# Gathered graph convolution: lists in pieces of 64 places for any set of 32-column groups, and half tiles on alternating pairs of banks

## The chip, the cores and the metric

The kernel runs on one core of a Trainium2 chip. The metric is the device time of one execution in microseconds; the time before is the median of three runs, 1504.62 us (1504.0 to 1505.56).

## The reference

`x` is [8, 4096, 256], `adj` [4096, 4096], `W` [256, 256], all float32.

```python
HW = jnp.einsum('bnf,fo->bno', H, W)
A_norm = jax.nn.relu((A + A.T) * 0.5)
D = jnp.sum(A_norm, axis=1)
D_safe = jnp.where(D > 0, D, 1.0)
d_inv_sqrt = jnp.where(D > 0, D_safe ** (-0.5), 0.0)
DAD = d_inv_sqrt[:, None] * A_norm * d_inv_sqrt[None, :]
L_norm = jnp.eye(N, dtype=H.dtype) - DAD
out = jnp.einsum('nm,bmo->bno', L_norm, HW)
return jax.nn.relu(out)
...
x = _layernorm(x + _L0_gnn_ref(x, L0_gnn_W, adj), axis=-1)
```

`adj` is sparse, with a density that falls with the row number: the first rows and columns hold most of the entries. Of the product with the Laplacian, only those rows matter that have an entry in the output block's columns.

## The kernel before, in words

**First stage (to about 582 us).** `adj` is read in blocks of 512 x 512, each is transposed (L515), added to its mirror (L519), put through a relu (L523) and stored in `a_dram`. For each row and each group of 32 columns a flag is kept (`uses`, L527) that says whether there is an entry. Beside that the product of x and W is formed (L615, L626) and stored in `g_dram`, one row of 2048 floats (8 batches x 256), 8 KB, for each node. Output block 0 is accumulated along the way (`lead`, L584). Lists for the first units are made here too.

**Second stage (from 582 us).** The remaining 31 blocks of 128 output columns are taken in 16 units of two blocks (b = 0 and 1; the last unit has one), in the order SEQ. A unit has eight groups of 32 columns, and the set of groups that a row has entries in is its mask, a number from 0 to 255. A unit needs the rows whose mask is not 0. They are placed in list tiles of 128 places, made of two halves of 64; KINDS gives fifteen masks that a half can stand for (single groups, pairs of groups, a whole block, and 0 for everything, "the rest"), CAPS how many halves each gets, FIRST where they begin. A row whose own kind is full goes to a wider one (`offer`, L334 on). For each tile POOL issues two indirect DMAs: the rows' piece of `a_dram`, 32, 128 or 256 columns wide (`ga`, L1031), and their rows of `g_dram` (`g`, L1039). Twelve tiles fit into SBUF (the ring); their slots are given back in the order of issue. The rows of the first 256 nodes, in which nearly all groups have entries, are not gathered: tiles 0 and 1 of `g_dram` are kept in SBUF (`g_hub`), and a unit with HUBS = 2 uses both, one with HUBS = 1 the first alone; their piece of `a_dram`, 64 KB, is loaded for each block (`gh`).

**The products (L1254).** A block's output is [128 columns, 2048], four PSUM banks c = 0 to 3 of 512 each, tag b0 or b1. `steps_of` plans a unit as a sequence of steps. A step fills the 128 columns of TensorE's array: one product of 128 x 128, or several narrower ones of different tiles beside each other; SHAPES lists the widths, and with 64 rows instead of 128 two products share the rows of the array, where half i always writes block i. In each step all products of bank 0 are issued, then those of bank 1, and so on. When block 0 of a unit is complete, `finish` evicts it (ACT, L787), adds the residual (DVE, L797), takes the moments (L806, L808), the inverse root and the normalisation (L830), and stores it.

**The lists** of the units to come are made in passing: `patterns` (L255 to L295) makes the masks and the indicator of each kind, 14 kinds x 32 node blocks = 448 columns; `count` (L299, L300) multiplies them on TensorE with a matrix of ones and a triangle, which gives each row's number within its kind; `place` (L302 to L390) turns it to a place; `count_rest` and `place_rest` (L395 to L419) do so for what is left over; `spread` (L428 to L444) and `collect` (32 small matmuls, L449) turn rows with places into places with rows, and `index` makes the addresses. `lists(u, room)` runs at the end of each unit's block 0: it takes three PSUM tiles of tag b0, issues the counts on TensorE for the third and fourth unit ahead, and the collect matmuls of the second ahead a few at a time between the steps (`thread`).

`queue(engine)` puts an instruction behind the last one issued on that engine, so the order of the program is the order on each queue.

## Time and profile before

| what | before |
|---|---|
| median of 3 runs (range) | 1504.62 us (1504.0 to 1505.56) |
| profiled execution (its span) | 1504.0 us |
| first stage / second stage | 582 us / 922 us |
| TensorE busy in the second stage | 867.87 us |
| VectorE busy in the second stage | 626.69 us |
| GpSimd busy in the second stage | 589.24 us |
| DMA share in the second stage | 0.94 |
| gathers (queue 0) | 53552 packets, 287.25 MB |

In the page, a group of instructions is one line of the program on one engine with its operands, count, busy time, mean time of one (ns) and the idle time of the engine just before. "PE" is TensorE, "PEld" its weight loads, "DVE" VectorE, "POOL" GpSimd. The chain is followed back from the last instruction to what released it, step by step, so its shares say what ended last, not what was busy. In the table of windows each engine has its busy time with the number of instructions in brackets, then TensorE's granted clock, the DMA share and the rate.

### The profile page before, as it was taken

How to read it: one execution, taken by the hardware profiler on the slowest of the kernel's cores; microseconds unless marked ns; L12 is line 12 of the kernel's file. 1: busy time of each engine (PE TensorE's matmuls, PEld its weight loads, DVE VectorE, ACT ScalarE, POOL GpSimd, SP SyncE). 2: the span in 40 equal slices, each digit the busy share in tenths (PEclk: the TensorE clock that was granted, in tenths of full speed). 3: DMA queues.
4: the chain of work that ended last, by engine and by line, in shares of the span. 5: the costliest groups of instructions: out<-in, count | busy, mean ns of one | idle time of the engine just before them, and what ended most of it. 6: DMA issues, size and time to landing. Idle time of an engine off the chain costs nothing.

```text
span 1504.0 us, 20175 instructions
## 1 busy us (share of the span) xinstructions
PE 1406.1 (93%) x6584; PEld 746.6 (50%) x6584; DVE 1028.0 (68%) x3020; ACT 369.3 (25%) x462; POOL 741.5 (49%) x1521
## 2 busy tenths in 40 slices
PE   7998998989999999989898989998999998999996
PEld 6777876767777764323333333333333333333342
DVE  4667579789597734147566776787989239999535
ACT  4555554544445440010100001001010010101102
POOL 2434010011223346756556776676666647567652
PEclk9999999989999999999999999999999999999999
DMA  9999999998999999969889999989999979999995
GB/s 359 349 377 380 402 390 358 394 362 319 400 358 332 364 418 367 377 263 362 338 304 358 334 393 349 373 336 396 413 380 357 408 278 395 382 383 404 409 389 207
DMA packets 215008, 545.83 MB, mean 363 GB/s; under 512 B 16983, under 2 KB 106647, under 8 KB 179879
## 3 DMA queue, kind: packets, MB, share of 16 engines
q0 software_dynamic: 53552, 287.25, 49.1%
q1 hardware_dynamic: 93200, 126.62, 24.3%
q10 hardware_dynamic: 68144, 130.58, 22.7%
q8 instruction: 55, 0.90, 0.2%
q14 instruction: 57, 0.47, 0.1%
HBM read 426.33 MB, written 136.34 MB: 374 GB/s over the span
## 4 chain that ended last, share of the span: by engine, by line
PE 60%; DVE 19%; DMA 12%; issue 5%; ACT 3%; POOL 1%; another core or an unknown queue 0%; ACTq 0%; DVEq 0%; POOLq 0%
PE py L1254 40%; PE pg L626 9%; DMA a_dram<-sym 7%; PE lead L584 5%; DVE sym L519 4%; DMA g<-g_dram,gi 3%; PE xtr L615 3%; PE tr L515 3%; ACT sym L523 2%; DVE stats L806 1%; DVE sums L526 1%; DVE hot L428 1%; DVE xr L830 1%; DVE xr L797 1%; DMA xin<-in_x_dram 1%
## 5 line engine op out<-in xcount | busy, mean ns | idle before, releaser
L1254 PE MATMUL py<-g,ga 128*128 128x512 f32 (+4 forms) x2808 | 678.4, 605 | 23.0 <-issue 16.1
L1254 PEld LDWEIGHTS py<-g,ga 128*128 128x128 f32 (+4 forms) x2808 | 236.6, 140 | 427.5 <-issue 401.1
L1039 POOL DMA_INDIRECT g<-g_dram,gi x257 | 297.4, 1157 | 149.4 <-issue 77.3
L1031 POOL DMA_INDIRECT ga<-a_dram,ai x257 | 269.6, 1049 | 159.8 <-issue 61.2
L787 ACT ACTIVATE y<-py,minus_r 128x512 f32<-128x512 f32 x120 | 80.4, 689 | 807.4 <-PE py L1254 644.7
L626 PE MATMUL pg<-w_sb,xt 128*128 128x256 f32 x1024 | 231.0, 384 | 7.1 <-ACT xt L616 7.1
L626 PEld LDWEIGHTS pg<-w_sb,xt 128*128 128x128 f32 x1024 | 195.3, 193 | 34.2 <-ACT xt L616 8.1
L519 DVE TENSOR_TENSOR sym<-tr,adj 128x512 f32<-128x512 f32 x256 | 162.4, 685 | 57.6 <-PE tr L515 51.2
L526 DVE TENSOR_REDUCE sums<-sym 128x64 f32<-128x2048 f32 x64 | 145.7, 2282 | 65.9 <-ACT sym L523 65.9
L1254 PE MATMUL py<-g_hub,gh 128*128 128x512 f32 x384 | 182.5, 616 | 5.5 <-issue 3.4
L527 POOL TENSOR_SCALAR uses<-sums 128x64 uint8<-128x64 f32 x64 | 26.7, 417 | 268.3 <-DVE sums L526 238.6
L515 PE MATMUL tr<-ident,adj 128*128 128x128 f32 x1024 | 136.9, 281 | 20.7 <-DVE sym L519 14.8
L523 ACT ACTIVATE sym<-sym 128x2048 f32<-128x2048 f32 x64 | 122.8, 1919 | 122.9 <-DVE sym L519 114.2
L515 PEld LDWEIGHTS tr<-ident,adj 128*128 128x128 f32 x1024 | 115.5, 143 | 51.1 <-DVE sym L519 32.1
L1254 PEld LDWEIGHTS py<-g_hub,gh 128*128 128x128 f32 x384 | 71.6, 194 | 111.7 <-issue 104.4
L241 DVE TENSOR_TENSOR_SCAN incl_r<-carry,lists 128x32 f32<-128x32 bf16 x13 | 2.8, 218 | 150.7 <-PE lists L396 147.1
L428 DVE TENSOR_TENSOR hot<-iota_q,at 128x1024 bf16<-128x1024 f32 x64 | 74.5, 1219 | 34.2 <-ACT y L787 32.1
L797 DVE TENSOR_TENSOR xr<-xr,y 128x2048 f32<-128x2048 f32 x31 | 70.8, 2284 | 39.6 <-ACT y L787 36.1
L615 PE MATMUL xtr<-ident,xin 128*128 128x128 f32 x512 | 74.0, 297 | 16.0 <-DVE sym L519 10.0
L830 DVE TENSOR_SCALAR xr<-xr,mv,root 128x256 f32<-128x256 f32 x248 | 85.5, 417 | 1.1
L806 DVE BATCH_NORM_STATS2 stats<-xr 128x6 f32<-128x256 f32 x248 | 84.0, 412 | 1.1
L584 PE MATMUL lead<-gt,strip 128*128 128x512 f32 x176 | 82.4, 593 | 0.0
(164 smaller groups left out, 1032.1 us busy)
## 6 DMA issues: line engine op xcount, KB each, us to landing
adj<-in_adj_dram SPq DMA_DIRECT2D x64, 1024.0 KB
a_dram<-sym ACTq DMA_DIRECT2D x64, 1024.0 KB
out_dram<-xr SPq DMA_DIRECT2D x31, 1024.0 KB
xr<-in_x_dram ACTq DMA_DIRECT2D x28, 1024.0 KB
xin<-in_x_dram SPq DMA_DIRECT2D x44, 512.0 KB
g_dram<-gt ACTq DMA_DIRECT2D x22, 1024.0 KB
xin<-in_x_dram POOLq DMA_DIRECT2D x20, 512.0 KB
g_dram<-held ACTq DMA_DIRECT2D x10, 1024.0 KB
```

What stands on the lines that cost most here:

```text
L515: ins = nc.tensor.transpose(pt[:, c * P : (c + 1) * P], tji[:, c, a * P : (a + 1) * P], ident)
L519: nc.vector.tensor_add(sym[:, a, :], pt, tij[:, a, :])
L523: nc.scalar.activation(sym, sym, AF.Relu, scale=0.5)
L526: nc.vector.tensor_reduce(sums, sym.rearrange("p a (c q) -> p a c q", q=E), AX.X, ALU.add)
L584: nc.tensor.matmul(lead[c], lhsT=strip, rhs=g[:, c * S : (c + 1) * S], start=not done, stop=len(done) == NB - 1, skip_group_check=True,)
L615: nc.tensor.transpose(pt[:, k, c, :], xin[b // H][:, b % H + k, c * P : (c + 1) * P], ident)
L626: ins = nc.tensor.matmul(pg[:, k * FO : (k + 1) * FO], lhsT=xt[:, b + k, c, :], rhs=w_sb[:, c, :], start=(c == 0), stop=(c == FC - 1),)
L806: nc.vector.bn_stats(stats[:, b, :], z[:, b, :])
L830: nc.vector.tensor_scalar(z[:, b, :], z[:, b, :], mv[:, b, 0:1], rstd[:, b : b + 1], ALU.subtract, ALU.mult,)
L1031: nc.gpsimd.indirect_dma_start(out=at if both else at[:, : E if one else P], out_offset=None, in_=a_pairs if both else a_groups if one els ...
L1039: nc.gpsimd.indirect_dma_start(out=gt, out_offset=None, in_=g_dram, in_offset=bass.IndirectOffsetOnAxis(ap=gi[:, t : t + 1], axis=0), boun ...
L1254: return nc.tensor.matmul(py[2 * u + 1 + b][c][cols, :], lhsT=at[ps, off + cols.start : off + cols.stop], rhs=gt[ps, c * S : (c + 1) * S], ...
```

## The change

The lists get a table of their own for each unit. PIECES names, in the order of the places, masks of any kind and how many halves of 64 each has; ORDER gives the sequence in which a unit's tiles are used. `Table` makes from them the kinds, the rest, and for each tile the width of its piece of `a_dram`. `choose` compares each row's mask with all masks of the table (up to 23) and takes the narrowest that holds it; the cascade of offers and the indicator with 448 columns go, and `count` is one matmul with at most 23 columns instead of two with 448. HUBS is 2 for all units. `spread` and `collect` leave out the hub rows (30 instead of 32 matmuls). `lists` takes one PSUM tile instead of three for the counts and the collected lists. Ring slots are given back in any order.

The planner puts products in full rounds ("F", 128 rows) and half rounds ("H", 64 rows, up to eight products beside each other, of any block). Half rounds are issued in groups of up to two. Each has two phases: in the first, products of one row half write banks 0 and 1 and those of the other write banks 2 and 3; in the second it is the other way round. Ahead of the second phases of a group an instruction on TensorE's queue waits for all half products so far. So two halves may now write the same block.

Counted in the program: list tiles 257 to 272, steps 226 to 211 (a half round of two phases counted as one), products of the second stage 1596 to 3472, half rounds 9 to 64 (52 of them with eight products to a bank), waits between phases 0 to 45.

```diff
-KINDS = [15, 1, 4, 2, 8, 16, 64, 32, 128, 240, 51, 204, 60, 195, 0]
...
-HUBS = [2, 2, 2, 1, 2, 2, 2, 1, 1, 2, 1, 1, 1, 1, 2, 2]
+HUBS = [2, 2, 2, 2, 2, 2, 2, 2, 2, 2, 2, 2, 2, 2, 2, 2]
...
+PIECES = [
+    [
+        (154, 2), (69, 2), (245, 2), (209, 1), (232, 1), (175, 1), (64, 2), (2, 3), (41, 2), (43, 1), (195, 1),
...
+ORDER = [
+    [8, 7, 19, 14, 6, 1, 13, 0, 20, 17, 21, 22, 5, 24, 10, 12, 4, 23, 16, 18, 2, 15, 9, 3, 11],
...
+    class Table:
+
+        def __init__(self, u):
+            full = 255 if blocks(u) == 2 else 15
+            self.pieces, at = [], {}
+            for mask, n in PIECES[u]:
+                if mask:
+                    at[mask] = len(self.pieces), n
+                self.pieces += [mask] * n
+            self.pieces += [0] * (len(self.pieces) % 2)
+            self.tiles = len(self.pieces) // 2
+            self.rest = at.pop(full)
+            self.kinds = [(m, *at[m]) for m in sorted(at, key=lambda m: (bits(m), m))]
+            self.places = [self.place(t, u) for t in range(self.tiles)]
+
...
+        def place(self, t, u):
+
+            a, b = self.halves(t)
+            a, b = a or b, b or a
+            if bits(a) == bits(b) == 1:
+                return E, [QU * (2 * u + 1) + m.bit_length() - 1 for m in (a, b)]
+            if all(not m & 15 or not m >> QU for m in (a, b)):
+                return P, [2 * u + 1 + int(not m & 15) for m in (a, b)]
+            return 2 * P, [u, u]
+
+    tables = [Table(u) for u in range(NU)]
...
+    def choose(u):
+
+        pat = plan[u]
+        n = len(tables[u].kinds)
+        ks = slice(kind_at[u], kind_at[u + 1])
+        all_ = [P, n, NB]
+        beyond = ipool.tile([P, kmax, NB], I16, tag="beyond", name=f"beyond_{u}", bufs=1)[:, :n]
+        nc.vector.tensor_tensor(
+            beyond,
+            pat.unsqueeze(1).to_broadcast(all_),
+            outside[:, ks].unsqueeze(2).to_broadcast(all_),
+            ALU.bitwise_and,
+        )
+        kind = ipool.tile([P, kmax, NB], BF16, tag="kind", name=f"kind_{u}", bufs=1)[:, :n]
+        nc.vector.scalar_tensor_tensor(
+            kind, beyond, 0.0, rank[:, :n].unsqueeze(2).to_broadcast(all_), ALU.is_equal, ALU.mult
+        )
+        best = ipool.tile([P, NB], F32, tag="best", name=f"best_{u}", bufs=1)
+        nc.vector.tensor_reduce(best, kind.rearrange("p k m -> p m k"), AX.X, ALU.max)
+        nc.vector.tensor_scalar(best, best, 1.0, None, ALU.max)
+        nc.vector.tensor_tensor(kind, kind, best.unsqueeze(1).to_broadcast(all_), ALU.is_equal)
...
+        plan[u] = pat, kind, incl, tot
...
+    def rounds_of(tiles, nb):
+
+        pend = [(t, set(cells_of(m0, m1, nb))) for t, m0, m1 in tiles]
+        rounds = []
+        while any(left for _, left in pend):
+            near = [p for p in pend if p[1]][:REACH]
+            wide, half = {}, {}
+            for p in near:
+                for b, e, k in sorted(p[1]):
+                    if k == 2:
+                        wide.setdefault(e, (p, b, e))
+                    else:
+                        half.setdefault((k, e), (p, b, e))
+            split = {e: wide[e] for e in wide if (0, e) not in half and (1, e) not in half}
+
+            def oldest(cells):
+                return 0.13 * any(p is near[0] for p, _, _ in cells)
+
+            score = len(wide) / QU + oldest(wide.values())
+            score_h = (len(half) + 2 * len(split)) / (2 * QU) if half else 0
+            score_h += oldest([*half.values(), *split.values()])
+            score_h -= 0.05 * (not rounds or rounds[-1][0] != "H")
+            if wide and score >= score_h:
+                for p, b, e in wide.values():
+                    p[1].discard((b, e, 2))
+                rounds.append(("F", [(p[0], None, b, e) for p, b, e in wide.values()]))
                 continue
+            cells = []
+            for (k, _), (p, b, e) in half.items():
+                p[1].discard((b, e, k))
+                cells.append((p[0], k, b, e))
+            for p, b, e in split.values():
+                p[1].discard((b, e, 2))
+                cells += [(p[0], k, b, e) for k in range(2)]
+            rounds.append(("H", cells))
+        return rounds
+
...
+    def phases_of(u, turn):
+
+        out = []
+        for kind, run in groupby(sequence(u), lambda r: r[0]):
+            run = list(run)
+            if kind == "F":
+                out += [(2, [(op, (0, 1, 2, 3)) for op in ops_of(cells, True)], False) for _, cells in run]
+                continue
+            for k in range(0, len(run), GROUP):
+                group = [ops_of(cells, False) for _, cells in run[k : k + GROUP]]
+                for back in range(2):
+                    for ops in reversed(group) if back else group:
+                        chunks = [(0, 1) if op[1] == turn[0] else (2, 3) for op in ops]
+                        out.append((1, list(zip(ops, chunks)), back == 1 and ops is group[-1]))
+                    if not back:
+                        turn[0] = 1 - turn[0]
+        return out
...
         def gather_ahead():
-            nonlocal asked, eaten
-            while eaten < asked and not uses_left[order[eaten]]:
-                eaten += 1
-            while asked < len(order) and asked - eaten < RING:
+            nonlocal asked
+            while asked < len(order) and free:
                 gather(asked)
                 asked += 1
...
         def lists(u, room):
 
-            tot, low, pr = (psum.tile([P, S], F32, tag="b0", name=f"lists{k}_{u}") for k in range(3))
-            tot, low = tot[:, : NL * NB], low[:, : NL * NB]
-            pl = pr[:, 2 * NB :]
-            pr = pr[:, : 2 * NB].rearrange("p (k m) -> p k m", k=2)
+            pl = psum.tile([P, S], F32, tag="b0", name=f"lists_{u}")
+            low, pr = pl[:, :kmax], pl[:, kmax : kmax + 2]
+            pl = pl[:, P:]
             reads = []
             with queue("pe"):
                 if 3 in ahead[u]:
-                    count_rest(ahead[u][3], pr[:, 0], pr[:, 1])
-                    reads.append(place_rest(ahead[u][3], pr[:, 0], pr[:, 1]))
+                    count_rest(ahead[u][3], pr[:, 0:1], pr[:, 1:2])
                 if 4 in ahead[u]:
-                    count(ahead[u][4], tot, low)
-                    reads.append(place(ahead[u][4], tot, low))
+                    n = len(tables[ahead[u][4]].kinds)
+                    count(ahead[u][4], low[:, :n])
+                    reads.append(place(ahead[u][4], low[:, :n]))
+            if 3 in ahead[u]:
+                in_turn(place_rest, ahead[u][3], pr[:, 0:1], pr[:, 1:2])
             for steps in reads:
                 in_turn(next, steps, None)
             if 2 in ahead[u]:
                 v = ahead[u][2]
-                pl = pl[:, : 2 * tiles[v]].rearrange("p (k t) -> p k t", k=2)
+                t = tables[v].tiles
+                pl = pl[:, : 2 * t].rearrange("p (k t) -> p k t", k=2)
...
+        def wait_for(products):
+
+            with queue("pe"):
+                mark = nc.tensor.nop().ins
+            for ins in products:
+                tc.add_manual_dep(
+                    mark,
+                    ins.name,
+                    mybir.DependencyInfo(mybir.DependencyClass.Sync, mybir.DependencyReason.DATA),
+                    reason="row tiles change banks",
                 )
 
...
+            if fresh:
+                wait_for(halves)
+                halves.clear()
+            first = [op for op, _ in ops if op[2] not in begun]
+            assert not first or [op[1:2] + op[3:] for op, _ in ops] == [(None, 0, QU)]
+            begun.update(touched)
+            for k in range(len(ops[0][1])):
+                for op, cs in ops:
+                    c = cs[k]
+                    for e in range(op[3], op[3] + op[4]):
+                        left[op[2], e, c] -= 1
+                    ends = all(not left[op[2], e, c] for e in range(op[3], op[3] + op[4]))
+                    ins = product(u, op, c, op in first, ends)
+                    if op[1] is not None:
+                        halves.append(ins)
+            for op, _ in ops:
                 t = op[0]
-                uses_left[u, t] -= 1
-                if t < 0:
-                    load_hub_rows(SEQ[SEQ.index(u) + 1 :], -1 - t, op[2])
```

TensorE, in unit 2 of the program (py_2 is that unit's accumulator: unit, block, bank; g and ga are the ring slots). Before, half products of four steps, where the first half writes block 0 and the second block 1:

```order
L1254 MATMUL py_2_0_0_6394<-g9_5749,ga9_5767 32x512 [waits DMASW1_49,DMASW0_49]
L1254 MATMUL py_2_1_0_6531<-g9_5749,ga9_5767 32x512
L1254 MATMUL py_2_0_0_6394<-g10_5753,ga10_5768 32x512 [waits DMASW4_49,DMASW3_49]
L1254 MATMUL py_2_1_0_6531<-g10_5753,ga10_5768 32x512
L1254 MATMUL py_2_0_0_6394<-g11_5757,ga11_5769 32x512 [waits DMASW6_49,DMASW5_49]
L1254 MATMUL py_2_1_0_6531<-g11_5757,ga11_5769 32x512
L1254 MATMUL py_2_0_0_6394<-g0_5713,ga0_5758 32x512 [waits DMASW7_49,DMASW0_49]
L1254 MATMUL py_2_1_0_6531<-g0_5713,ga0_5758 32x512
```

After, the last bank pair of a first phase, then (behind six collect matmuls, cut here) the second phase, whose first product has the wait ahead of it:

```order
L1231 MATMUL py_2_1_1_6639<-g8_5802,ga8_5823 32x512
L1231 MATMUL py_2_1_1_6639<-g5_5790,ga5_5820 32x512
L1231 MATMUL py_2_1_1_6639<-g11_5814,ga11_5826 32x512
L1231 MATMUL py_2_1_1_6639<-g8_5802,ga8_5823 32x512
...
L1231 MATMUL py_2_1_0_6638<-g2_5778,ga2_5817 32x512 [waits PE_49]
L1231 MATMUL py_2_1_0_6638<-g5_5790,ga5_5820 32x512
L1231 MATMUL py_2_1_0_6638<-g11_5814,ga11_5826 32x512 x2
L1231 MATMUL py_2_1_2_6640<-g8_5802,ga8_5823 32x512
L1231 MATMUL py_2_1_2_6640<-g5_5790,ga5_5820 32x512
L1231 MATMUL py_2_1_2_6640<-g11_5814,ga11_5826 32x512
```

Both halves now write block 1, in different banks, and the exchange of banks stands behind a wait on TensorE itself.

TensorE at the end of a unit's block 0, where the lists of later units are counted and collected. Before:

```order
L395 LDWEIGHTS ones
L395 MATMUL lists_2_6659<-rest_6369,ones 128x32 [waits Activation_49]
L396 LDWEIGHTS lower
L396 MATMUL lists_2_6659<-rest_6369,lower 128x32
L299 LDWEIGHTS ones
L299 MATMUL lists_2_6657<-kind_5986,ones 128x448 [waits Activation_49]
L300 LDWEIGHTS lower
L300 MATMUL lists_2_6658<-kind_5986,lower 128x448 [waits Activation_49]
L449 LDWEIGHTS hot_6384 [waits DVE_49]
L449 MATMUL lists_2_6659<-val_6386,hot_6384 128x36 [waits DVE_49]
```

After:

```order
L402 LDWEIGHTS lower_86
L402 MATMUL lists_2_6937<-tot_r_5_6536,lower_86 128x1 [waits Activation_49]
L403 LDWEIGHTS ones_87
L403 MATMUL lists_2_6937<-tot_r_5_6536,ones_87 128x1
L369 LDWEIGHTS lower_86
L369 MATMUL lists_2_6937<-tot_6_6636,lower_86 128x15 [waits DVE_49]
L454 LDWEIGHTS hot_4_6548
L454 MATMUL lists_2_6937<-val_4_6550,hot_4_6548 128x36 [waits DVE_49]
```

The wide counts are gone, and the first collect matmul now writes the tile that VectorE reads the counts from.

VectorE at the same place, ahead of which the collect matmul waits. Before:

```order
L241 SCALAR_TENSOR_TENSOR incl_r6_7120<-carry_96,lists2_3_7115 128x32 [waits PE_49]
L245 TENSOR_TENSOR pos_r6_7122<-incl_r6_7120,lists2_3_7115 128x32 [waits DVE_49]
L246 TENSOR_TENSOR pos_r6_7122<-pos_r6_7122,lists2_3_7115 128x32 [waits DVE_49]
L241 SCALAR_TENSOR_TENSOR incl_k7_7125<-carry_96,lists0_3_7113 128x448 [waits PE_49]
L245 TENSOR_TENSOR pos_k7_7127<-incl_k7_7125,lists0_3_7113 128x448 [waits DVE_49]
L246 TENSOR_TENSOR pos_k7_7127<-pos_k7_7127,lists1_3_7114 128x448 [waits DVE_49,PE_49]
L797 TENSOR_TENSOR xr_7_7006<-xr_7_7006,y_7_7092 128x2048 [waits DMAHW4_49,DMAHW0_49,Activation_49]
```

After:

```order
L409 TENSOR_SCALAR over_125<-lists_2_6937 128x1 [waits PE_49]
L410 TENSOR_SCALAR incl_r_5_6534<-incl_r_5_6534,lists_2_6937 128x32
L412 SCALAR_TENSOR_TENSOR fits1_5_6943<-incl_r_5_6534,rest_5_6532 128x32 [waits DVE_49]
L413 SCALAR_TENSOR_TENSOR incl_r_5_6534<-incl_r_5_6534,fits1_5_6943 128x32 [waits DVE_49]
L414 TENSOR_TENSOR slot_5_6528<-slot_5_6528,incl_r_5_6534 128x32 [waits DVE_49]
L416 TENSOR_SCALAR ip_5_6947<-slot_5_6528 128x32 [waits DVE_49]
L420 TENSOR_SCALAR digit_5_6949<-ip_5_6947 128x32 [waits DVE_49]
L421 CAST at_5_6950<-digit_5_6949 128x32 [waits DVE_49]
L422 TENSOR_SCALAR digit_5_6949<-ip_5_6947 128x32 [waits DVE_49]
L423 CAST at_5_6950<-digit_5_6949 128x32 [waits DVE_49]
L378 TENSOR_TENSOR at_k_6_6955<-lists_2_6937,base_101 128x15
```

Before, the tile of the rest and of the collected lists (lists_2) had its last reader in the third operation; after, the one tile has it in the eleventh.

657 lines of the change are left out of this document (278 added, 379 removed), and 47 rows, old and new, of tables (CAPS, FIRST, ORDER).

## The prediction

> **What bounds the kernel now.** I read the page first, for the span and the busy shares, then the table of windows for the two stages, and then the chain of what ended last in three stretches of the second stage.
>
> ```profile
> span 1504.0 us, 20175 instructions
> PE 1406.1 (93%) x6584; PEld 746.6 (50%) x6584; DVE 1028.0 (68%) x3020; ACT 369.3 (25%) x462; POOL 741.5 (49%) x1521
> q0 software_dynamic: 53552, 287.25, 49.1%
> ```
>
> ```profile
> core 0: us, PE busy (x) PEld busy (x) DVE busy (x) ACT busy (x) POOL busy (x), PEclk, DMA share, GB/s
> 0.00:582.00 582.00, 538.22 (x2893) 420.61 (x2894) 401.36 (x768) 280.55 (x328) 152.22 (x967) 0.97 1.00 371
> 582.00:1504.00 922.00, 867.87 (x3693) 325.99 (x3691) 626.69 (x2252) 88.78 (x134) 589.24 (x555) 0.97 0.94 358
> ```
>
> The span is the profiled execution's whole time; the median of the timed runs, 1504.62 us, lies 0.6 us above it, and I add that at the end. In the first stage (to 582 us) the DMA engines are busy for 1.00 of the time, so what the change does there to TensorE and VectorE is hidden; I take that stage as it is. In the second stage TensorE is busy for 867.87 of 922 us and the DMA share is 0.94: two limits that are only 54 us apart. The chain tells which of them ends last, by stretches (582 to 922, 922 to 1262, 1262 to 1492):
>
> ```profile
> by line: PE py L1254 92.1%; issue 5.4%; PE lists L449 1.3%; PE lead L584 0.4%; DVE incl_r L241 0.3%; DVE pos_r L245 0.3%; DVE pos_r L246 0.3%; PE lists L396 0.1%; PE lists L395 0.1%
> ```
>
> ```profile
> by line: PE py L1254 51.8%; DMA g<-g_dram,gi 6.2%; DVE hot L428 4.0%; DVE stats L806 4.0%; DVE xr L830 4.0%; issue 3.7%; DVE xr L797 3.3%; another core or an unknown queue 1.1%; DVE incl_k L241 0.9%; DVE slot L386 0.8%; DVE mv L808 0.8%; DV
> ```
>
> ```profile
> by line: PE py L1254 47.1%; DMA g<-g_dram,gi 11.4%; issue 10.0%; POOL g L1039 4.8%; POOL ga L1031 3.7%; DMA ga<-a_dram,ai 2.9%; DVE stats L806 2.5%; DVE xr L830 2.4%; DVE hot L428 2.0%; DVE xr L797 1.9%; PE lists L449 0.7%; DVE g L1108 0.5%
> ```
>
> So the units that run up to 922 us are bound by the products of TensorE; behind that, products hold about half of the chain and the rest is split between VectorE and the gathers. A TensorE term counts in full at first and less later.
>
> **Part by part: steps and half tiles.** A step of four full products is eight matmul records in a row; where two of them stand between pieces of other work, each takes 3.52 us, and a step in which each quarter of the columns is another tile's costs the same. The windows hold single steps, in this order: eight half products to a bank (two rows), six to a bank, four quarter products of 128 rows (two rows).
>
> ```profile
> 648.09 3.52 PE py L1254 x8
> 651.62 0.27 PE lists L449 x11
> 651.89 3.52 PE py L1254 x8
> ```
>
> ```profile
> 636.51:643.12 6.61, 6.40 (x65) 1.65 (x64) 0.00 (x0) 1.85 (x3) 1.95 (x2) 1.00 0.77 316
> 713.59:718.53 4.94, 4.82 (x65) 1.62 (x64) 0.00 (x0) 1.85 (x3) 0.94 (x1) 1.00 1.02 428
> 847.17:850.75 3.58, 3.58 (x50) 1.01 (x48) 0.00 (x0) 0.93 (x2) 2.70 (x3) 1.00 0.94 329
> 855.80:859.38 3.58, 3.58 (x34) 1.66 (x29) 3.44 (x4) 0.00 (x0) 2.73 (x3) 1.00 0.88 295
> 643.12:646.69 3.57, 3.57 (x34) 0.94 (x32) 0.00 (x0) 0.69 (x1) 0.00 (x0) 1.00 0.00 0
> ```
>
> From the two planners' tables I count 226 steps before and 211 after (a half round of two phases counted as one step, hub steps included), with 14 more hub steps among the 211: 15 steps fewer at 3.53 us is **-53 us**. In exchange the after kernel has 64 half rounds where the before had nine, and 52 of the 64 have eight half products to a bank. Their price is the open size of this case. The six-op row says 3.58 us, nothing extra; the two eight-op rows say 1.37 and 3.04 us extra. In both of these the first two of the four banks run at full pace, then a few records come about 0.7 us apart, and then the pace is full again. The chain shows the same crawl from 666 us on, in a step of 128-row quarter products and the hub step behind it, so it is not proven to belong to half products:
>
> ```profile
> 638.98 2.06 PE py L1254 x7
> 641.04 0.12 issue
> ...
> 666.17 0.10 issue
> 666.27 0.59 PE py L1254
> 666.86 0.12 issue
> 666.98 0.61 PE py L1254
> 667.59 0.85 issue
> 668.44 0.59 PE py L1254
> ```
>
> I take 0.5 us for each of the 52, a good third of the smaller of the two rows, since the row of six stands at nothing: **+26 us**, with ends 0, +71 (1.37 each) and +158 (3.04 each).
>
> The Trainium skill speaks to this on the page "TensorE: Matmul & The Clock Gate", section "Packing small matmuls — row/col tiling": tiles of the array that don't collide overlap within its 64-deep window, and a pack takes one matmul's time plus about 4 ns for each further tile. By that rule the 26 us would be zero; the six-op row agrees, the two eight-op rows do not.
>
> **The waits between phases.** Each group of half rounds (45 of them, 26 with one round and 19 with two) gets an instruction on TensorE's queue that waits for all half products issued so far, before the row halves swap their pairs of banks. Behind it are queued that group's remaining products, the list matmuls threaded between them, and so the eviction and the release of ring slots. A wait of this kind is not in the trace. From below stand the short "issue" pieces of the chain (0.10 to 0.12 us above), from above one of them plus one matmul that has to run out, 605 ns by the mean of the products' row:
>
> ```profile
> L1254 PE MATMUL py<-g,ga 128*128 128x512 f32 (+4 forms) x2808 | 678.4, 605 | 23.0 <-issue 16.1
> L1254 PE MATMUL py<-g_hub,gh 128*128 128x512 f32 x384 | 182.5, 616 | 5.5 <-issue 3.4
> ```
>
> I take 0.4 us, the middle, 45 times: **+18 us** (5 to 32). Switching between full and half rows is in that figure.
>
> On the page "TensorEngine Tiling (Array Packing)", section "Key Properties", the Trainium skill says that a change of tiling mode, not only of the tile, drains the TensorE. That speaks against a change that switches so often; but the step of 3.57 us in the windows' last row starts where the eight-op step of the first row ends, and it is no longer than the other of its kind, so no such drain shows here.
>
> **The list machinery.** Two 448-column count matmuls per unit go (12 units) for one of at most 23 columns: 24 x 0.35 us = **-8.4 us**. But all parts of a unit's lists now share one PSUM tile, so the first collect matmul waits for VectorE's last reader of that tile, and products queue behind it on TensorE. Before, three short operations stood there:
>
> ```profile
> L300 PE MATMUL lists<-kind,lower 128*128 128x448 bf16 x12 | 4.2, 350 | 0.0
> ...
> L418 DVE TENSOR_SCALAR digit<-ip 128x32 int32<-128x32 int32 x13 | 2.7, 207 | 2.7 <-DVE at L417 2.4
> L410 DVE TENSOR_TENSOR slot<-slot,pos_r 128x32 f32<-128x32 f32 x13 | 2.5, 196 | 3.1 <-DVE pos_r L407 2.8
> ```
>
> ```profile
> 722.32 0.23 DVE incl_r L241
> 722.57 0.20 DVE pos_r L245
> 722.79 0.20 DVE pos_r L246
> 722.99 0.04 issue
> ```
>
> That is 0.63 us. After, ten operations of place_rest and one of place stand there, of the kinds that take 0.16 to 0.21 us: about 2.3 us, 1.7 more, 13 times: **+22 us**. Below it could be 0 where VectorE is done long before TensorE arrives; above it could be 13 x 3.7 = 48, if each grows to the longest wait of this kind that there is now:
>
> ```profile
> PE lists L449 <- DVE pos_r L246: 11.8, 11, 4.3
> ```
>
> The 448-column operations on VectorE are fewer and the cascade of offers goes:
>
> ```profile
> L241 DVE TENSOR_TENSOR_SCAN incl_k<-carry,lists 128x448 f32<-128x448 bf16 x12 | 13.0, 1080 | 0.3 <-PE lists L300 0.3
> L386 DVE TENSOR_REDUCE slot<-pos_k 128x32 f32<-128x448 f32 x12 | 11.1, 928 | 0.4
> L383 DVE TENSOR_TENSOR pos_k<-pos_k,fits 128x448 f32<-128x448 f32 x12 | 7.6, 630 | 0.4
> ```
>
> Before, a unit's lists take a scan, a reduction and six operations of 448 columns by these rows (5.8 us), and the half-width and small ones of the cascade and the patterns, some 17 us as I estimate it; after, about seven operations of up to 22 x 32 elements at 0.6 to 0.7 us, a scan of 1.1, two reductions of 1.0 and the small ones, some 11 us: 12 x 6 = 70 us less busy. VectorE holds about a fifth of the chain in the middle stretch and less than that in the last, so I count a fifth: **-14 us** (0 to -30).
>
> **Transfers.** Fifteen more tiles, but pieces of 64 places let 703 fewer rows be gathered (30,655 to 29,952 counted from the input, 8 KB each, 5.76 MB). Queue 0 spends 49.1% of 1504 us on 287.25 MB, 2.57 us a MB: -14.8 us; 14 hub loads of 64 KB (0.9 MB) give 2.4 back. Of 12.4 us I count half, as the gathers end last only in the later stretches: **-6 us** (0 to -12). Two more POOL issues for each of 15 tiles cost what these rows say:
>
> ```profile
> L1039 POOL DMA_INDIRECT g<-g_dram,gi x257 | 297.4, 1157 | 149.4 <-issue 77.3
> L1031 POOL DMA_INDIRECT ga<-a_dram,ai x257 | 269.6, 1049 | 159.8 <-issue 61.2
> ```
>
> 15 x 2.2 = 33 us beside 589 busy of 922: hidden while ring slots are free; without that cover they cost their 33. Slots now come free in any order, so an early half tile no longer holds back those behind it; what that gains is in no row (0 to the 6% that g holds in the middle stretch, 21 us) and I count nothing.
>
> Sum: -53 + 26 + 18 - 8.4 + 22 - 14 - 6 = -15.4 us, so 1488.6 us against the profiled 1504.0, and 1489 with the 0.6 us to the median.
>
> **The rivals.**
> *R1, half rounds at the pace of the eight-op rows (slower).* The place is each half round with eight products to a bank. At 1.37 us extra the term is 71 instead of 26: 1489 + 45 = 1534 us; at 3.04 it would be 1621. It decides from (15 + 26) / 52 = 0.8 us a round. For it: both such steps that I looked at were slow. Against: the crawl shows elsewhere too, and half of each step ran at full pace.
> *R2, half rounds at full pace.* The six-op row holds for eight: 1489 - 26 = 1463 us. It is also what the packing rule cited above gives.
> *R3, the gathers take over.* TensorE's saving is hidden because transfers already fill 0.94 of the stage; then between 1504 - 12 = 1492 and 1504 us, about 1498. For it: the last stretch's 11.4% for g, and POOL lines in the chain. Against: the first 340 us are 92% products.
> That the change does not do what it says can be left out: the steps and waits are counted in the instruction order itself.
>
> **How the numbers follow.** Forecast 0.36 (1489 us, 1470 to 1506 by its own terms), R1 0.30, R2 0.20, R3 0.14. A measurement of this kernel tells 0.2%, 3 us. Faster: 0.33 of the forecast, all of R2, 0.04 of R3: 0.57. Same: 0.02 and 0.06: 0.08. Slower: 0.01, 0.30 and 0.04: 0.35. The range takes in R2 with some of its terms' slack at the low end and R1 at its smaller price at the high end, 1455 to 1540; what is left out is R1 at the price of the larger row and R2 with the VectorE and transfer terms at their best.
>
> **What would show it.** In the after profile: single half rounds of eight in the windows, 3.6 us (R2), about 4 (forecast) or 5 and more (R1); TensorE's idle time before the instruction behind each wait (0.4 us); the wait of the collect matmuls for VectorE (about 2.3 us, 13 times); the DMA share of the second stage (R3: 0.97 or more). The forecast is wrong if TensorE's products take the same total with fewer steps, or if gathers end last in the first stretch too.

## The result, and the profile after

The changed kernel takes 1707.7 us (median of four, 1700.69 to 1708.74) against 1504.31 us (four, 1501.71 to 1505.56): ratio 1.1342, 95% interval 1.1302 to 1.1381. It is 203 us slower; 15 us faster was forecast.

The page of the profiled execution, 1708.74 us:

```profile
span 1707.0 us, 27320 instructions
PE 1473.3 (86%) x10288; PEld 715.4 (42%) x10288; DVE 956.5 (56%) x2425; ACT 368.1 (22%) x462; POOL 752.9 (44%) x1809
q0 software_dynamic: 56768, 283.20, 46.0%
```

The table of windows, in the same columns as before:

```profile
0.00:582.00 582.00, 533.19 (x2866) 418.32 (x2867) 391.10 (x633) 278.86 (x326) 138.67 (x1204) 0.96 0.99 365
582.00:1707.00 1125.00, 940.10 (x7424) 297.11 (x7422) 565.45 (x1792) 89.26 (x136) 614.23 (x606) 0.90 0.83 293
```

All of the loss is in the second stage, 922 to 1125 us. The transfers did not become the limit: their share fell from 0.94 to 0.83. VectorE has 61 us less to do, where 70 was worked out. TensorE is busy 72 us more with 15 steps fewer, and idle 131 us more (54 to 185). Its products by shape in that stage, after and then before (busy us, mean ns, idle time ahead of them and who ended it):

```profile
L1231 PE MATMUL py<-g,ga 64*32 64x512 f32 x3912 | 342.2, 678 | 105.6 <-remote 79.6 <-issue 11.3 <-PE py L1231 9.5
L1231 PE MATMUL py<-g,ga 128*32 128x512 f32 x2464 | 325.2, 628 | 12.8 <-issue 11.6
L1231 PE MATMUL py<-g_hub,gh 128*128 128x512 f32 x496 | 224.5, 608 | 7.5 <-DVE low L469 7.5
```

```profile
L1254 PE MATMUL py<-g,ga 128*32 128x512 f32 x1056 | 147.5, 609 | 22.1 <-issue 15.6 <-DMA g<-g_dram,gi 6.0
```

The idle time stands ahead of the half products, and its largest releaser is called "remote": the view finds no instruction that set the semaphore. The view of TensorE's waits says so too (us in all, times, longest). In the chain from 960 to 1340 us the same wait holds 31%, under the name "another core or an unknown queue":

```profile
PE py L1231 <- remote: 79.6, 18, 12.3
PE lists L454 <- DVE at_k L378: 22.9, 6, 10.1
```

```profile
by line: PE py L1231 46.7%; another core or an unknown queue 31.3%; issue 4.0%; DVE hot L433 2.2%; DMA ga<-a_dram,ai 2.2%; DVE stats L802 2.1%; DMA g<-g_dram,gi 2.1%; DVE xr L826 2.1%; DVE xr L793 1.8%; PE lists L454 1.3%; DVE incl L356 0.7
```

There is one core. The instruction that waits here is the new one between the phases, and what it waits for is TensorE's own half products. TensorE's timeline shows it (start us, duration, work, and in brackets the idle time before it):

```profile
754.88 4.86 PE L1231 MATMUL py<-g,ga 128*32 128x512 f32 x32
759.67 0.45 PE L454 MATMUL lists<-val,hot 128*128 128x36 bf16 x11
760.05 1.95 PE L1231 MATMUL py<-g,ga 64*32 64x512 f32 x32
761.93 0.34 PE L454 MATMUL lists<-val,hot 128*128 128x36 bf16 x6
768.76 1.96 PE L1231 MATMUL py<-g,ga 64*32 64x512 f32 x16 [6.48 <-remote]
```

The first row is a step of four quarter products of 128 rows: 4.86 us where 3.6 was counted. Here that is the granted clock (the third figure from the end), which is about half of the full one for the first 2.62 us:

```profile
754.88:757.50 2.62, 2.62 (x19) 0.67 (x20) 2.58 (x3) 0.00 (x0) 0.00 (x0) 0.52 0.91 291
757.50:762.00 4.50, 4.50 (x70) 1.31 (x63) 4.26 (x22) 0.00 (x0) 1.69 (x2) 1.00 0.32 122
762.00:768.76 6.76, 0.28 (x7) 0.15 (x7) 3.96 (x15) 0.00 (x0) 4.17 (x5) 0.66 0.89 322
```

The third row of the timeline is the first phase of a half round of eight, two banks in 1.95 us, all records done at 762.0; and yet the wait for those products ends at 768.8 (the trace has the update of their semaphore at 768.7). So these products are recorded at full pace and are finished late (the profile models the end of a matmul and does not measure it, so a record can end before its product does). That is the cost, and the experiments ask what makes it.

One thing must be known ahead to read them: the same kernels gave other times in other sets of runs (the kernels of one set share a chip), each steady within itself, in us:

| set | before (runs) | changed kernel (runs) |
|---|---|---|
| first timing | 1504.31 (4) | 1707.7 (4) |
| A: e1 to e4 | 1469.86 (7) | (only with own tile, 1497.57) |
| B: e5 to e8 | 1469.91 (7) | 1499.39 (4) |
| C: e9, e10 | 1467.98 (1), profiled 1476.6 | 1490.22 (1) |
| D: e11, e12 | 1497.35 (8) | |
| E: e13 to e16 | 1504.58 (1) | 1684.6 (1) |

In A, B and C the change costs 1 to 2%; in the first timing and E it costs 12 to 13%. I call what is added there the stall. B and E carry the same chip number, and the runs don't say whether that is the same chip, so whether the stall hangs on the chip or on its condition stays open. Each experiment below is compared inside its set, unless it is said otherwise.

The traces show one more difference between the sets, and it goes with the stall. For the same program the packed trace of e10 holds 15361 semaphore updates that came from DMAs, and that of the first timing 10940; for the kernel before these are 14719 in e9 and 10638 in the first timing, for the kernel of e4 and e14 15368 and 10690. So the traces of the sets that stall lack records which the others have, and a wait can stand under "issue" or "remote" in their views for that alone. Each run on record lists a granted clock, so each was recorded, and whether the recording takes part in the stall was not tested.

### The profile page after: what moved, and what is told of

Read it like the earlier page. It is cut to its first block, busy times and chain, and to the rows that moved or that the text cites. A ratio compares the mean times of both kernels' runs of the same rounds, so it can differ in the third digit from the quotient of the medians.

```text
span 1707.0 us, 27320 instructions
## 1 busy us (share of the span) xinstructions
PE 1473.3 (86%) x10288; PEld 715.4 (42%) x10288; DVE 956.5 (56%) x2425; ACT 368.1 (22%) x462; POOL 752.9 (44%) x1809
## 3 DMA queue, kind: packets, MB, share of 16 engines
q0 software_dynamic: 56768, 283.20, 46.0%
## 4 chain that ended last, share of the span: by engine, by line
PE 60%; DVE 14%; another core or an unknown queue 11%; DMA 9%; issue 4%; ACT 2%; POOL 0%; ACTq 0%; DVEq 0%; POOLq 0%
PE py L1231 40%; PE pg L623 8%; DMA a_dram<-sym 7%; PE lead L581 5%; DVE sym L516 3%; PE xtr L612 3%; PE tr L512 3%; DVE sums L523 1%; DVE stats L802 1%; ACT sym L520 1%; DMA g<-g_dram,gi 1%; DVE xr L826 1%; PE lists L454 1%; DVE xr L793 1%
## 5 line engine op out<-in xcount | busy, mean ns | idle before, releaser
L1231 PE MATMUL py<-g,ga 64*32 64x512 f32 (+1 forms) x6448 | 693.5, 658 | 118.4 <-remote 79.6
L1231 PEld LDWEIGHTS py<-g,ga 64*32 64x32 f32 (+1 forms) x6448 | 183.4, 116 | 592.0 <-issue 450.3
L1005 POOL DMA_INDIRECT ga<-a_dram,ai x272 | 278.8, 1025 | 305.2 <-PE py L1231 205.1
L1013 POOL DMA_INDIRECT g<-g_dram,gi x272 | 299.6, 1102 | 136.5 <-issue 79.6
L1231 PE MATMUL py<-g_hub,gh 128*128 128x512 f32 x496 | 224.5, 608 | 7.5 <-DVE low L469 7.5
L1231 PEld LDWEIGHTS py<-g_hub,gh 128*128 128x128 f32 x496 | 94.4, 195 | 127.2 <-issue 116.9
L433 DVE TENSOR_TENSOR hot<-iota_q,at 128x768 bf16<-128x768 f32 (+1 forms) x64 | 70.0, 1152 | 33.6 <-issue 32.1
L581 PE MATMUL lead<-gt,strip 128*128 128x512 f32 x176 | 86.7, 614 | 0.0
```

Of the source, the lines that this page charges most:

```text
L581: nc.tensor.matmul(lead[c], lhsT=strip, rhs=g[:, c * S : (c + 1) * S], start=not done, stop=len(done) == NB - 1, skip_group_check=True,)
L1005: nc.gpsimd.indirect_dma_start(out=at[:, :w], out_offset=None, in_=a_dram.rearrange("j (c q) -> (j c) q", q=w), in_offset=bass.IndirectOff ...
L1013: nc.gpsimd.indirect_dma_start(out=gt, out_offset=None, in_=g_dram, in_offset=bass.IndirectOffsetOnAxis(ap=gi[:, t : t + 1], axis=0), boun ...
L1231: return nc.tensor.matmul(py[2 * u + 1 + b][c][cols, :], lhsT=at[rows, off + cols.start : off + cols.stop], rhs=gt[rows, c * S : (c + 1) * S],
```

## The experiments

**Is it the shared PSUM tile, or a TensorE term at all? (A)** e1 gives the collected lists a PSUM tile of their own:

```diff
-            pl = pl[:, P:]
+            pl = psum.tile([P, S], F32, tag="b0", name=f"lists1_{u}")
```

> The changed kernel, but the collected lists have a PSUM tile of their own again, apart from the one of the counts. In the changed kernel the collect matmuls waited about 45 us in all for VectorE's readers of the shared tile (at_k, digit, end_k: 22.9 + 5.9 + 4.4 + 7.3 us and a few small ones). If the list tile is a cause by itself, those waits fall to about 10 us and the time falls by 30 to 50 us, more if each of these idle times also costs a stretch at half clock behind it (then up to 80). If the half products stall the array whatever stands between them, only the 30 us or less come off and about 170 us of the loss stay: 1660 to 1685 us. If the list waits only cover stalls that come anyway, nothing changes (1700 or more).

e2 is the changed kernel and e3 the kernel before, both without the 8 KB gathers of `g` behind the first twelve tiles (the products then use stale rows):

```diff
-            with queue("pool"):
+            if n < RING:
+              with queue("pool"):
```

> The changed kernel without the 8 KB gathers behind the first twelve tiles (the products read what stands in the ring, so the output is not the reference's). If gather traffic holds up TensorE, the late ends of the products (up to 12 us behind their dispatch) go, and the second stage comes near the products' own time, about 211 steps x 3.6 = 760 us and the lists' waits, 820 us, so about 1400 us. If the half products or the waits between phases are slow by themselves, the second stage stays above 1000 us and the waits behind half products stay as long: 1600 us or more.

> The kernel before, with the same gathers left out (output not the reference's). Its 226 steps x 3.55 are 802 us against a second stage of 922. If gather traffic causes its crawls (65 us) and waits, the second stage falls to about 830 us and the total to about 1410; if not, it stays above 890 us, and the total above 1470.

e4 makes each half product one of 128 rows, which computes more than is wanted: 270 full rounds, no half round and no wait between phases.

```diff
-                    out.append((b, e, 2 if all(two) else two.index(1)))
+                    out.append((b, e, 2))
```

> The changed kernel with each half product made a 128-row product of the same tile (it also takes in the rows of the other half, so the output is not the reference's): no half rounds, no phases and no waits between them, but 270 full rounds in the place of 147 and 64 half rounds. At 3.6 us that is 59 rounds or 212 us more work for TensorE. If half products (or their waits) hold up the array, this costs no more than the changed kernel: 270 x 3.6 = 972 us, the before's loss of 120 us and 45 us of list waits, about 1720 us, with a granted clock of 0.95 or more. If the loss has nothing to do with half products (gathers, lists, hubs), it stays and the 212 us come on top: over 1820 us.

Measured: e1 1497.57 us (ratio 1.0162, 1.0111 to 1.0213), e2 1416.52, e3 1429.9, e4 1650.8 (1.1228, 1.1178 to 1.1277). e1 is 28 us behind the kernel before and not 200. e1 and e4 lie below all their marks, which were worked out from the first timing. e4's 12% is the price of whole rows: its products of 32 columns run without a pause (its rows stand below), but a half product made whole takes twice its place, 270 steps instead of 211. Without the gathers the changed kernel is 13.4 us faster than the other. The second stages of e2 and of e3:

```profile
582.00:1414.50 832.50, 778.39 (x7411) 263.37 (x7409) 562.47 (x1792) 89.69 (x136) 320.78 (x340) 0.99 0.38 112
```

```profile
582.00:1428.20 846.20, 822.47 (x3685) 311.81 (x3683) 618.36 (x2250) 89.47 (x132) 304.57 (x308) 0.99 0.34 106
```

TensorE is busy 44.1 us less (15 steps at 3.53 are 53), but idle 30 us more. Of e2's 54 us of idle time the collect matmuls have 28:

```profile
PE lists L454 <- DVE at_k L378: 18.1, 8, 2.4
PE lists L454 <- DVE end_k L380: 9.5, 4, 2.4
```

**Did e1 take the 200 us away? (B)** The changed kernel itself, with nothing edited (e5), beside e1's kernel again (e6), the changed kernel with `GROUP = 1`, so 64 waits and not 45 (e7), and one in which the products of a phase are sorted so that those of one row half no longer come in a run (e8):

```diff
+                        pairs.sort(key=lambda at: (at[0][3], at[0][1], at[0][2]))
```

> The changed kernel as it is, once more, beside the kernel with the own list tile on the same chip. In the run with the own tile the waits ahead of the second phases were 0.06 to 0.3 us each, 6 us in all, against 92 us in the profile of the changed kernel, which ran on another chip. If the shared tile's waits start the stalls (an idle stretch, half clock, and so on), the changed kernel is 150 to 200 us slower than the own-tile one here too, ratio to before 1.12 to 1.14. If the late ends of the half products belong to the first chip, only the list waits themselves separate the two: 40 to 60 us, ratio 1.04 to 1.06.

> The own-tile kernel again, for the difference to the changed kernel on one chip: ratio to before 1.01 to 1.02 as in its first run if it does not hang on the chip; 1.08 or more if this chip stalls half products.

> The changed kernel with each half round in a group of its own: 64 waits between phases in the place of 45, each right behind the phase it waits for, and everything else the same. If a wait costs a drain of 0.1 to 0.3 us, 19 more of them cost 3 to 6 us and nothing is to be seen beside the changed kernel. If each wait costs what it cost in the first profile (92 us for 45, 2 us each), 39 us come on top, and more with the clock.

> The changed kernel with the eight products of a phase issued in turns of the two row halves (column group by column group) and not four of one half and then four of the other. If the order of the pack decides whether the array keeps up, the late ends of half products go and the time falls by the loss they cause (100 us on a chip that shows it); if not, the time is that of the changed kernel within 5 us.

Measured: e5 1499.39 us (1.0205, 1.0157 to 1.0252), e6 1499.13 (1.0188, 1.0136 to 1.0239), e7 1494.77 (1.0153, 1.0115 to 1.0191), e8 1494.42 (1.0154, 1.0093 to 1.0216). The unedited kernel ran without the stall, so e1 had cured nothing; own tile, more waits and another order in the pack make no difference that these runs can tell. In e6 another wait stands where the collect matmuls' was:

```profile
PE py L1231 <- DVE low L470: 21.9, 6, 4.0
```

**Where are the 1.5 to 2%? (C)** Both kernels unedited, profiled in one set.

> The kernel before, for a trace on the chip that this call gets. On the chip of the last two calls its median was 1470 us, against 1504 where the change was first timed. If that is the crawl of TensorE (65 us of products 0.7 us apart in the first trace, with the data there in time), the crawl is under 30 us here and the second stage 885 to 890 us, with a DMA share of 0.95 or more: the gathers bound it. If the difference lies elsewhere (first stage, transfers), the crawl is as long as before.

> The changed kernel beside it, to tell on which kind of chip this call runs: about 1499 us with waits of 0.1 us ahead of second phases, or about 1707 us with waits of 2 us. Where the gathers bound both kernels, its DMA-busy time in the second stage is at least as long as that of the kernel before, although it moves 4 MB less in queue 0; if it is shorter, the time it loses is TensorE's.

Measured: 1476.6 and 1490.22 us. The second stage, queue 0 and TensorE's waits, e9 and then e10:

```profile
582.00:1474.90 892.90, 850.56 (x3706) 324.85 (x3704) 623.90 (x2252) 92.25 (x136) 597.05 (x560) 0.99 0.97 372
...
q0 software_dynamic: 53552, 287.25, 49.3%
...
PE py L1254 <- DMA g<-g_dram,gi: 19.6, 13, 3.4
```

```profile
582.00:1488.50 906.50, 817.14 (x7410) 271.73 (x7408) 564.96 (x1792) 89.76 (x136) 631.63 (x601) 0.97 0.97 361
...
q0 software_dynamic: 56768, 283.20, 50.0%
...
PE py L1231 <- DMA g<-g_dram,gi: 37.7, 24, 3.9
PE lists L454 <- DVE at_k L378: 23.5, 10, 2.5
PE py L1231 <- PE py L1231: 0.7, 3, 0.3
```

Without the stall the transfers are the nearer limit for both kernels: the DMA share is 0.97 in both, and in set A leaving out the gathers made the kernel before 40 us faster (1469.86 to 1429.9) and the changed one 81 (e1 to e2, with other list tiles). TensorE is busy 33 us less and the stage is 14 us longer. DMA time is 0.97 x 892.9 = 866 us before and 0.97 x 906.5 = 879 after, 13 more (the share has two digits, so some 5 us either way), though 4 MB less are moved on queue 0: a MB there costs 49.3% x 1474.9 / 287.25 = 2.53 us before and 50.0% x 1488.5 / 283.20 = 2.63 after. The wait between phases hardly shows: 0.7 us in all. The place of the first timeline, in e10:

```profile
714.37 3.64 PE L1231 MATMUL py<-g,ga 128*32 128x512 f32 x32
717.94 0.45 PE L454 MATMUL lists<-val,hot 128*128 128x36 bf16 x11
718.32 1.95 PE L1231 MATMUL py<-g,ga 64*32 64x512 f32 x32
720.20 0.32 PE L454 MATMUL lists<-val,hot 128*128 128x36 bf16 x6
720.45 1.95 PE L1231 MATMUL py<-g,ga 64*32 64x512 f32 x32
```

The quarter step takes 3.64 us and not 4.86 (here at full clock), and the second phase follows 0.18 us after the first and not 6.8.

**Do two kept tiles cost it, or the gathers? (D)** e11 is the kernel before with HUBS = 2 for all units (240 steps), e12 the changed kernel with own tile and without the gathers of `g` (e1's and e2's edits together).

```diff
-HUBS = [2, 2, 2, 1, 2, 2, 2, 1, 1, 2, 1, 1, 1, 1, 2, 2]
+HUBS = [2, 2, 2, 2, 2, 2, 2, 2, 2, 2, 2, 2, 2, 2, 2, 2]
```

> The kernel before with one part of the change alone: two kept tiles in all units (HUBS all 2), its own lists and steps otherwise. 14 hub steps more (240 steps in the place of 226), 14 hub loads of 64 KB more, and the rows of nodes 128 to 255 drop out of the gathers of seven units. If the gathers bound the kernel on ordinary chips, the fewer rows pay: 0 to 12 us faster than before. If TensorE bounds it, 14 steps x 3.53 = 49 us come on top, up to 1520 us.

> The changed kernel with the own list tile and without the 8 KB gathers (output not the reference's): TensorE and the lists alone. Against 1416.5 us with the shared tile: if the collect waits cost what they show (28 us in that trace), 1388 to 1392; if VectorE's index operations only take their place, 1405 or more. On a chip that stalls (before at 1504 us), a time under 1420 says that the stalls come from the gathers' traffic, and over 1500 that they come from TensorE's products alone.

Measured: e11 1509.12 us (1.0094, 1.0058 to 1.0130), 12 us slower than the kernel before in its set, so the kept tiles are not the 13%. e12 took 1453.1 us, between its two marks, where e2 took 1416.52 in set A. Its second stage, and the half products of e12 and then of e2:

```profile
582.00:1451.00 869.00, 809.28 (x7410) 270.90 (x7408) 560.69 (x1792) 88.41 (x136) 333.38 (x341) 0.98 0.36 108
...
L1232 PE MATMUL py<-g,ga 64*32 64x512 f32 x3912 | 264.1, 603 | 24.8 <-remote 12.4 <-PE py L1232 6.7 <-issue 2.4
```

```profile
L1232 PE MATMUL py<-g,ga 64*32 64x512 f32 x3912 | 242.0, 596 | 4.9 <-PE py L1232 0.7
```

The DMA share is 0.36, and TensorE is still busy 31 us more than in e2; with their idle time the half products take 42 us more, and the waits for "remote" are there. So the stall does not need the gathers of `g`, though it is smaller here than the 200 us. (e2 has no list tile of its own, and both are single runs of two sets.) The kernel before is slower in set D as well (1497 against 1470 us), and e11, which differs from it in HUBS alone, has 14.2 us of idle time ahead of products that wait for no semaphore; e9 has none, and the first timing's trace of the kernel before 17.3. So the stall is there too. The set has no run of the unedited changed kernel, so how much of the difference is the set's own is not known.

**Half rounds, waits, or narrow products? (E)** e13 is the changed kernel unedited and e14 the kernel of e4. In e15 the next full round is issued between the two phases of a group, so that the wait stands one step later:

```diff
+                        if k + GROUP >= len(run) and n + 1 < len(runs):
+                            out.append(wide(runs[n + 1][1].pop(0)[1]))
```

e16 is the kernel of e8.

> The changed kernel again. On a chip where the kernel before takes 1497 us or more I expect about 1700 us, with waits of 2 us ahead of second phases and products that end several us behind their dispatch; on one where it takes 1470, about 1495 us.

> All half products as 128-row products (output not the reference's; 270 full rounds, no waits between phases). On a stalling chip: if products of two row halves side by side (or the waits behind them) cause the stalls, it is at most as slow there as the changed kernel and hardly slower than on the chip that gave 1651 us (up to 1700); if narrow products of 128 rows stall too, it is over 1750 us. On an ordinary chip: 1645 to 1655.

> The changed kernel with the next full round issued between the two phases of a group, so that the wait comes 3.6 us later, when the half products should long be done. On a stalling chip: if the idle stretch at the wait is what costs (clock, restart), most of the loss goes, 1550 us or less; if the half products themselves end late, the wait moves but stays, and the time is within 30 us of the changed kernel's. On an ordinary chip: within 5 us of it.

> The eight products of a phase in turns of the two row halves. On a stalling chip: if the order in the pack decides, under 1600 us; if not, within 30 us of the changed kernel. On an ordinary chip 1490 to 1500.

Measured: e13 1684.6 us, e14 1772.62, e15 1686.63, e16 1701.98, the kernel before 1504.58. The stall is back. e14 decides that the stall needs neither half rounds nor the wait: it is e4's kernel, which has neither, and it takes 122 us more. The groups of e4 and then of e14:

```profile
L1231 PE MATMUL py<-g,ga 128*32 128x512 f32 x6040 | 691.1, 594 | 0.0
L1231 PE MATMUL py<-g_hub,gh 128*128 128x512 f32 x496 | 238.3, 637 | 41.9 <-DVE low L470 41.9
```

```profile
L1231 PE MATMUL py<-g,ga 128*32 128x512 f32 x6040 | 769.5, 596 | 30.0 <-issue 25.3 <-DMA ga<-a_dram,ai 0.7
L1231 PE MATMUL py<-g_hub,gh 128*128 128x512 f32 x496 | 241.9, 645 | 37.2 <-DVE low L470 37.2
```

The narrow products (32 columns) take 691.1 us in the one and 769.5 + 30.0 in the other, 108 us more; the hub products, which fill all 128 columns, 280.2 and 279.1 with their idle time. The same 40 us of both timelines, e4 and then e14:

```profile
601.80 38.55 PE L1231 MATMUL py<-g,ga 128*32 128x512 f32 x354
```

```profile
601.16 1.31 PE L1231 MATMUL py<-g,ga 128*32 128x512 f32 x3 [0.24 <-issue]
602.63 0.59 PE L1231 MATMUL py<-g,ga 128*32 128x512 f32 x1 [0.15 <-issue]
604.04 1.02 PE L1231 MATMUL py<-g,ga 128*32 128x512 f32 x2 [0.82 <-issue]
605.48 1.02 PE L1231 MATMUL py<-g,ga 128*32 128x512 f32 x3 [0.42 <-issue]
606.94 19.47 PE L1231 MATMUL py<-g,ga 128*32 128x512 f32 x171 [0.44 <-issue]
```

In e4, 354 records without a gap; in e14 single records with gaps, for which no releaser shows, and then full pace again: the crawl that stood in the trace of before. It isn't data that comes late: by the trace the products of the first three of these rows wait for no semaphore. Nor is it a lower clock: the granted clock (the third figure from the end) is 1.00 in this stretch of e14.

```profile
600.00:640.00 40.00, 35.22 (x264) 16.09 (x259) 7.87 (x18) 0.00 (x0) 23.97 (x26) 1.00 0.97 368
```

From its first record's start to its last one's end, a step of four tiles takes 3.62 us in e4 and 4.37 on average in e14. Steps overlap a little; from one step's start to the next one's it is 3.53 and 4.14 us, and the 177 such steps make 624 us and 733, 109 more.

In e13 the waits for "remote" are long again, and in e15 they are mostly gone, without a gain (1686.63 against 1684.6). e13's row and then e15's:

```profile
PE py L1231 <- remote: 65.2, 16, 13.3
```

```profile
PE py L1237 <- DVE low L470: 27.7, 6, 11.0
PE py L1237 <- issue: 26.5, 58, 1.5
PE py L1237 <- remote: 11.9, 4, 4.9
```

So the wait only collects what the products ahead of it are late: with the wait moved away, the lateness shows elsewhere, as longer waits for VectorE and as small pauses (single runs). e16 shows that another order in the pack does not take the stall away.

## Why the prediction was wrong

**The step that failed** is "I take 0.5 us for each of the 52, a good third of the smaller of the two rows, since the row of six stands at nothing". It gave 26 us to half rounds, and 18 more to the waits behind them. In the first timing the half products take 342.2 + 105.6 = 447.8 us with their idle time, 222 more than 64 rounds at 3.53 us (226), where 26 + 18 = 44 was counted. The mechanism was wrong as well: the price was put on half rounds with eight products to a bank, but e14 shows a stall of narrow products of any kind, and it was at work in the trace from which the price was taken (the 208 records of 64-row, 32-column products take 18.6 us there and 14.6 in e9). The prediction quoted the crawl in a step of 128-row quarter products and wrote that it "is not proven to belong to half products", but it gave that no term and no rival. The change raises the records of 32-column products in the second stage from 1264 (1056 of 128 rows, 208 of 64) to 6376. The first timing against set B splits the 203 us: 29 are what the change costs without the stall, and 174 come from it, as the kernel before loses 1504 - 1470 = 34 us by it and the changed kernel 1707.7 - 1499.4 = 208. Scaled by the records alone, the 34 us would have become 171, if all of them come from narrow products. That is not shown: against e9 the row of 128 x 32 products is 18 us longer in the first timing, with its idle time, and that of the hub products 12. That set B's 1499 us lies near the forecast of 1489 is chance, as the kernel before takes 1470 there.

**Where the stall lies.** The second stage of the first timing's trace is 218 us longer than e10's. e10's groups, to be held against those of the first section with busy and idle time together:

```profile
L1231 PE MATMUL py<-g,ga 128*32 128x512 f32 x2464 | 292.3, 608 | 11.8 <-DMA g<-g_dram,gi 11.7
L1231 PE MATMUL py<-g,ga 64*32 64x512 f32 x3912 | 265.5, 612 | 30.3 <-DMA g<-g_dram,gi 26.0 <-PE py L1231 0.7
L1231 PE MATMUL py<-g_hub,gh 128*128 128x512 f32 x496 | 219.8, 597 | 4.5 <-DVE low L470 4.5
```

Half products: 447.8 against 295.8 us, 152 more; quarter products 338.0 against 304.1, 34 more; hub products 232.0 against 224.3, 8 more; the rest is with the lists and in small pauses. R1 was the nearest rival, and the larger of the two eight-op rows the one to believe for this condition, though even its price (52 x 3.04 = 158) is under the 222 us. R1's mechanism was too narrow, as e14 shows, and its 1621 us too low. For one round, the half products lose 152 / 64 = 2.4 us, the quarter products 34 / 77 = 0.4, and those of e14, where no half rounds are, 109 / 177 = 0.6. Whether half rounds stall more by themselves stays open, since a wait ahead of half products also collects what quarter products ahead of them owe.

**The clock.** The granted clock of the second stage is 0.90 in the first timing and 0.97 in e10, for which the prediction has no term. By the clock records of the traces TensorE is busy for 158 us at half clock in the one and for 41 in the other. If work goes with the clock, as in the first step of the first timeline (4.86 - 0.48 x 2.62 = 3.6 us, its length at full clock), that is an estimate of (158 - 41) / 2 = 58 of the 218 us. It does not start the stall where the traces can tell: e14 crawls at a clock of 1.00, and at the wait of the first timeline the clock is 1.00 when the wait begins and falls within it.

**The other steps.**
- *Fifteen steps, -53, and list counts, -8.4:* right without the stall. e2 against e3 has TensorE busy 44.1 us less. -53 - 8.4 leaves +17 for the half rounds, where 26 was taken, so without the stall that term was nearly right. By the Trainium skill's packing rule, which the prediction cited from "TensorE: Matmul & The Clock Gate", section "Packing small matmuls — row/col tiling", seven further tiles at 4 ns in each of a round's eight packs (four banks, two records for each product) give 0.22 us, an estimate of 12 us for 52 rounds, and not zero as the prediction had it. The +17 of set A is near that; the first timing and set E are not.
- *Waits between phases, +18:* too high without the stall (0.7 us in e10's waits; 64 in place of 45 cost nothing in e7). With it, the row reads 79.6 us, but e15 shows that this is the lateness of the products and not the wait's own price.
- *Collect waits, +22:* right where nothing stalls (2.3 us each was forecast, and e2's two rows are 27.6 us in 12 waits), but e6 beside e5 shows that removing them gains nothing: another wait on VectorE comes in their place, and the transfers are near their limit anyway.
- *VectorE, -14:* VectorE is busy 61 us less, and no experiment shows a gain from it.
- *Transfers, -6:* wrong in sign. Without the stall it is R3's place, transfers as the limit, but at 13 us more, not 6 less: each MB of queue 0 takes 4% longer with 56768 packets than with 53552. R3 had the saving hidden and no loss. Why a MB takes longer was not tried, and the rest of the 29 us by which the change is slower in set B is not assigned.

## What to carry to other kernels

Price a change by the shapes it multiplies: where a trace shows a crawl in some kinds of steps, count how many steps of those kinds the change adds, also if the crawl can't be explained, and give that a rival of its own. A saving in steps counted in full-pace time is worth what it says only where the new steps run at full pace, and a second set of runs of the kernel before can show whether the first ones did. Before a faster engine is credited, look at the limit right behind it, here a DMA share of 0.94 that became 0.97 when TensorE wasn't stalled.

## What the runs showed of the hardware that was not expected

Steps of 32-column products of 128 rows, four tiles beside each other, take about the time of a full product in e4 (3.62 us each) and 4.37 on average in e14, the same kernel in another set, while full-width products take the same in both. It isn't the granted clock: e4's second stage has 0.97 and e14's 0.96, which is 12 us of 120. A product's record can be at its end several microseconds before the semaphore of that product tells so (6.8 us at 762 us of the changed kernel's trace). What stalls, why some sets have it and others don't, whether the recording takes part, and why it is smaller without gathers (e12) stays open. No complete version of the change beats the kernel before in its own set: the best two of those run more than once, e7 and e8, stand at 1.015.
